# Decoder of two layers on one core: seven block products for the keys and values of the last cross-attention

## The chip, the cores and the metric

The kernel runs on one core of a Trainium2 chip. The metric is the device time of one execution in microseconds (us). TensorE (PE) multiplies matrices, its weight loads are listed apart as PEld; VectorE (DVE), ScalarE (ACT) and GpSimd (POOL) work on elements; SyncE (SP) issues most of the DMAs. All data is fp32.

## The reference

The input x has 8 batches of 256 tokens with 256 features. Two layers follow, each of a self-attention, a cross-attention and a feed-forward part with experts, each behind a layernorm and added to x:

```python
x = x + _L0_attn_ref(_layernorm(x), ...)
x = x + _L0_xattn_ref(ctx_2048, _layernorm(x), ...)
x = x + _L0_ffn_ref(_layernorm(x), ...)
x = x + _L1_attn_ref(_layernorm(x), ...)
x = x + _L1_xattn_ref(_layernorm(x), ctx_2048, ...)   # the change is here
x = x + _L1_ffn_ref(_layernorm(x), ...)

def _L1_xattn_ref(x, context, Wq, Wkv, null_kv, Wout, ln_scale, ln_bias):
    q = _split_heads(einsum('bnd,df->bnf', x, Wq))          # 16 heads of 64
    k, v = split(einsum('bmc,cf->bmf', context, Wkv), 2)    # context 256 x 512, Wkv 512 x 2048
    # a null key and value are put in front of k and v
    attn = softmax(einsum('bhid,bhjd->bhij', q * scale, k))
    out = einsum('bhij,bhjd->bhid', attn, v) @ Wout
    return (out - mu) * rsqrt(var + EPS) * ln_scale + ln_bias
```

The last part, `_L1_ffn_ref`, has one shared expert for all tokens and eight routed ones, of which each token takes the best.

## The kernel before

The program is unrolled. Up to about 620 us on the profile's clock it runs the first layer and the second layer's self-attention; then `null_cross_attention` (L1043) handles the cross-attention with heads of 64, one batch after another; from about 1173 us `token_experts` (L1273) runs the rest of the shared expert and the routed ones. The change lies in the middle part.

**Matmuls.** `product` (L272) splits the 128 output rows in two halves of 64 and issues a matmul for each, so its weight loads have 64 columns. In the trace each fp32 `nc.tensor.matmul` shows as two instructions.

**A batch b of the middle part.** A loop over b in `null_cross_attention` does the following.
- `weighted` (L1092) takes the keys kT, the values v and the queries qT of batch b. For each pair of heads it makes the scores (tile stx, in one of two double banks of the pool `scp`, tag "sc"), ACT takes their exponential into pTx (four buffers, tag "pT"), POOL adds two halves of it (both), TensorE sums these into the denominators (den) and multiplies pTx with the values (ox); ACT and DVE copy ox to oT.
- `layernorm_T` (L262) makes the transposed normed rows xnT of batch b+1, and `routed_norm` and `routed_rows` (L950, L964) those of batch b-1 for the experts; both end in transposes on TensorE and a copy on ACT.
- `reciprocals` (L1152) adds the null key's part to den, takes the reciprocal on DVE, writes it to DRAM (rd) and reads it back spread over the partitions (rs), both on SP's queue.
- `keys` (L1058) loads the transposed context ctxT of batch b+1 on SP's queue and multiplies it with the first half of wkv_x: for each two of the eight feature chunks, four contraction chunks with a moving operand of 256 tokens, and a copy of 512 columns on ACT (tile fm, kTx). `vals` (L1065) does it with the second half, context as weights and 512 features moving (vps, vx).
- `routed_scores` (L967) makes the routing scores of batch b-1.
- `divide` (L1184) multiplies oT by rs in four parts, two on POOL and two on DVE. `outward` (L1190) multiplies by Wout (tile wo), copies, normalises and adds to x, the last steps on DVE and POOL.
- `queries` (L1082) makes the null key's scores (nps) and the eight chunks of qT for batch b+1, copied by DVE.

Before the loop, keys, values and queries of batch 0 are made, and `load_shared` (L1222) loads the router and the shared expert's weights: `w_in` (L896) issues two DMAs on SP and a copy of the tail columns on POOL, `w_out` (L909) two DMAs, `ended` (L904) a memset on POOL. In batch 7 there are no keys to make: the weights wkv_x and wq_x are given up (`wproj.close()`), the tables of the routing are made on POOL, and the first quarter of the shared expert (tile hx) takes the place of keys and values.

**The order.** A planner (the tile framework) orders the instructions of each engine by priority, which is the order of the program text, and by its own estimate of when each can start. Within `tc.manual_schedule(engines=...)` the engines named keep the order of the text. Before, that holds for TensorE from batch 7 on (L1236). The planner also sets the waits: a write waits for earlier reads of the same tile where they overlap. TensorE's banks: `mm` has three single banks, `scp` two double ones, `op` one. Each engine handles its queue in order.

## Time and profile before

| | |
|---|---|
| Time, median of 3 runs | 1397.39 us (1395.36 to 1399.26) |
| The profiled execution, its own time | 1396.5 us |
| Its span, first to last instruction | 1394.8 us |
| TensorE busy | 97% of the span, 12198 matmul instructions |
| VectorE, ScalarE, GpSimd busy | 36%, 33%, 28% |
| Mean granted TensorE clock | 0.994 of full speed |
| The middle part, batch to batch | 63.7 us |

A line of the timeline has the start in us, the length in us of the merged run of instructions, the engine, the source line, the operation, output<-inputs by the names of the program, the shapes and the number of instructions; then, in brackets, how long the engine sat idle before it and what ended that. "128*64 128x256" on TensorE is a weight of 128 rows and 64 columns and 256 moving columns. The lengths of TensorE's runs include a modelled end of the last matmul, so neighbours overlap a little; differences of starts are free of that. A line that begins with a source line and ends in times "first to last" is from the view of one tile. PEclk is the granted clock in tenths, 9 for 90% or more, over 40 slices of the span.

### The profile page before, as it was taken

The numbers are of one execution on the slowest core, as the hardware profiler recorded it, in microseconds if no ns is written. First come the engines' busy times: TensorE is split into PE (matmuls) and PEld (weight loads), VectorE is DVE, ScalarE is ACT, GpSimd is POOL, SyncE is SP. The second block draws the span as 40 slices with busy tenths as digits, with TensorE's granted clock in tenths as the row PEclk, the third lists the DMA queues.
The fourth block names the chain that finished last, engine by engine and source line by source line (L and its number), as shares of the span: only waits on it lengthen the run. The fifth ranks groups of instructions, "written<-read, shape, count | busy, mean of one in ns | idle before, by whom it ended". The sixth has DMA issues, their size and how long they took to land.

```text
span 1394.8 us, 28640 instructions
## 1 busy us (share of the span) xinstructions
PE 1357.5 (97%) x12198; PEld 884.4 (63%) x12198; DVE 502.4 (36%) x1467; ACT 457.4 (33%) x730; POOL 395.7 (28%) x499
## 2 busy tenths in 40 slices
PE   6999999999999999989999999999999999999998
PEld 3666756756766666665655656565656555688884
DVE  5443563563565654330222213131312225422213
ACT  2555444444444434431222313131322222122221
POOL 4222142052033234220332415152423412400004
PEclk9999999999999999999999999999999999999999
DMA  8960000000000006010101010110101010779954
GB/s 312 345 205 16 9 24 9 8 24 1 1 9 2 2 9 221 1 53 26 32 16 31 16 47 2 46 32 16 32 1 32 1 31 5 283 289 414 402 209 127
DMA packets 46921, 116.56 MB, mean 84 GB/s; under 512 B 8273, under 2 KB 30401, under 8 KB 42433
## 3 DMA queue, kind: packets, MB, share of 16 engines
q1 hardware_dynamic: 38912, 92.74, 19.3%
q0 software_dynamic: 5152, 18.89, 3.6%
q10 hardware_dynamic: 2720, 3.02, 0.6%
q8 instruction: 98, 1.61, 0.5%
q14 instruction: 39, 0.31, 0.1%
HBM read 104.00 MB, written 27.93 MB: 95 GB/s over the span
## 4 chain that ended last, share of the span: by engine, by line
PE 85%; DVE 5%; POOL 4%; issue 1%; ACT 1%; DMA 0%; ACTq 0%; POOLq 0%; DVEq 0%; SPq 0%
PE fm L274 12%; PE st L332 9%; PE o L364 9%; PE vps L274 8%; PE h L274 6%; PE wo L274 4%; PE ox L1138 4%; PE stx L1100 4%; PE out L1475 3%; PE out L1292 3%; PE h L947 3%; PE qk L274 3%; PE hx L947 3%; PE tr L281 3%; PE den L1114 2%; PE ao L274 2%
## 5 line engine op out<-in xcount | busy, mean ns | idle before, releaser
L364 PE MATMUL o<-pT,padv 128*64 128x256 f32 (+1 forms) x1536 | 171.6, 365 | 1.1 <-POOL pT L344 1.1
L341 ACT ACTIVATE pT<-st 128x1024 f32<-128x1024 f32 (+1 forms) x128 | 110.5, 915 | 88.8 <-PE st L332 87.9
L364 PEld LDWEIGHTS o<-pT,padv 128*64 128x64 f32 x1536 | 103.1, 137 | 52.7 <-issue 10.0
L332 PE MATMUL st<-qm,kT 64*128 64x256 f32 (+1 forms) x1024 | 117.2, 367 | 0.9 <-DVE qm L310 0.6
L274 PE MATMUL fm<-ctxT,wkv_x 128*64 128x256 f32 x1024 | 112.9, 380 | 0.0
L274 PE MATMUL vps<-wkv_x,ctxT 128*64 128x512 f32 x512 | 111.8, 593 | 0.0
L332 PEld LDWEIGHTS st<-qm,kT 64*128 64x128 f32 x1024 | 90.1, 189 | 26.0 <-issue 15.6
L274 PEld LDWEIGHTS fm<-ctxT,wkv_x 128*64 128x64 f32 x1024 | 73.0, 137 | 37.3 <-issue 1.3
L1106 POOL TENSOR_TENSOR both<-pTx 128x512 f32<-128x512 f32 x64 | 79.6, 1273 | 57.4 <-ACT pTx L1104 33.8
L1104 ACT ACTIVATE pTx<-stx 128x1024 f32<-128x1024 f32 x64 | 62.1, 1021 | 89.9 <-PE stx L1100 86.8
L274 PE MATMUL h<-xrT,w 128*64 128x128 f32 (+1 forms) x1936 | 86.9, 250 | 1.4 <-issue 1.4
L274 PEld LDWEIGHTS h<-xrT,w 128*64 128x64 f32 x1936 | 84.3, 137 | 4.4 <-issue 2.1
L274 PEld LDWEIGHTS vps<-wkv_x,ctxT 128*64 128x64 f32 x512 | 36.4, 137 | 68.9 <-issue 68.6
L341 ACT ACTIVATE pT<-st,kbias 128x1024 f32<-128x1024 f32 x64 | 68.0, 1113 | 28.7 <-PE st L332 28.7
L256 POOL TENSOR_TENSOR lnrs<-lnve,mhalf 128x2 f32<-128x2 f32 x48 | 34.2, 717 | 147.0 <-DVE lnve L254 95.2
L332 PE MATMUL st<-qm,memk 64*128 64x256 f32 x512 | 68.8, 393 | 0.5
L939 ACT ACTIVATE sl<-h 128x128 f32<-128x128 f32 (+1 forms) x114 | 35.4, 310 | 96.1 <-PE h L274 56.7
L1100 PE MATMUL stx<-qTx,kTx 64*128 64x256 f32 x512 | 64.3, 391 | 2.5 <-ACT pTx L1104 2.5
L940 DVE TENSOR_TENSOR midr<-sl,h 128x128 f32<-128x128 f32 x102 | 29.4, 288 | 100.5 <-PE h L274 68.6
L251 DVE BATCH_NORM_STATS2 lxst<-yx 128x6 f32<-128x256 f32 x16 | 6.0, 418 | 162.7 <-ACT yx L1198 162.7
L274 PE MATMUL qk<-l_wqkv,xnT 128*64 128x512 f32 x256 | 62.6, 610 | 0.7 <-ACT xnT L284 0.7
L344 POOL TENSOR_SCALAR_AFFINE_SELECT pT<-pT 128x512 f32<-128x512 f32 x64 | 39.5, 638 | 83.1 <-ACT pT L341 79.8
(274 smaller groups left out, 2080.7 us busy)
## 6 DMA issues: line engine op xcount, KB each, us to landing
w<-packs SPq DMA_DIRECT2D x22, 1408.0 KB
w<-packs SPq DMA_DIRECT2D x22, 768.0 KB
rs<-rd SPq DMA_DIRECT2D x16, 512.0 KB
packs<-L_ffn_w_eDF SPq DMA_DIRECT2D x8, 704.0 KB
packs<-L_ffn_w_eDF SPq DMA_DIRECT2D x8, 640.0 KB
packs<-L_ffn_w_eFD SPq DMA_DIRECT2D x8, 640.0 KB
ctxT<-ctx_T SPq DMA_DIRECT2D x8, 512.0 KB
wkv_x<-L_xattn_Wkv POOLq DMA_DIRECT2D x1, 4096.0 KB, 17.3
```

The lines of the kernel that those rows point to most:

```text
L274: nc.tensor.matmul(out[h], lhsT[:, h], rhs, start=start, stop=stop, skip_group_check=True)
L281: nc.tensor.transpose(ps[:, c, t * P : (t + 1) * P], rows[:, t, c * P : (c + 1) * P], ident)
L332: nc.tensor.matmul(st[:, g, i, :n], kT[rows, c, bass.ts(kt, P)], qm[rows, 2 * mq + i, c, q0:], start=True, stop=True,)
L341: nc.scalar.activation(pT[:, :, :, :n], st[:, :, :, :n], AF.Exp, scale=scale, **kb)
L364: nc.tensor.matmul(o[64 * i : 64 * i + 64, mq, q0:], v_pad[:, kt, 4 * c + 2 * mq + i, 2 * g : 2 * g + 2, :], pTs[kt][:, g, i, : S - q0], s ...
L947: nc.tensor.matmul(h, shared["ws13"][:, c, lo : lo + P], shared["xnT"][:, c, bass.ts(q, 2 * S)], start=c == 0, stop=c == 1)
L1100: nc.tensor.matmul(st[:, g, kt, :], kT[rows, c, bass.ts(kt, P)], qT[rows, c, :], start=True, stop=True)
L1104: nc.scalar.activation(pT, st, AF.Exp, scale=scale)
L1106: nc.gpsimd.tensor_tensor(both, pT[:, :, 0, :], pT[:, :, 1, :], ALU.add)
L1138: nc.tensor.matmul(o[XD * g : XD * (g + 1), i, :], v[:, kt, 2 * (c2 + i) + g, :], pT[:, g, kt, :], start=kt == 0, stop=kt == 1, skip_group ...
L1292: nc.tensor.matmul(ps, mid[:, i, lo : lo + P], w2[:, i, :], start=i == 0, stop=i == NFC - 1)
L1475: nc.tensor.matmul(ps[h], mid[:, i, h], sets[k % len(sets)][1][:, i, :], start=i == 0, stop=i == NFC - 1, skip_group_check=True,)
```

## The change

For batches 1 to 7 the keys and the values are made by seven products of blocks in place of eight (Winograd's form of Strassen's scheme). The context is cut in two halves of tokens and two of its 512 features, each half of Wkv in two halves of its rows and two of its columns. Sums of the blocks of Wkv are made once by DVE, in 16 instructions of 512 columns, 12 of them behind batch 0's keys and 4 behind its queries; one overwrites a block of wkv_x. Sums of the blocks of ctxT are made by DVE for each batch, in four instructions of 256 columns (`sums_of_context`). `seven` makes the products in two banks xb and yb of one "sc" tile and a third bank zb from `mm`, so that three banks' sums serve four results: per seven, four copies on ACT (three into pT buffers, one into the result) and three adds on DVE. It is a generator that stops between products. For the keys a product is four feature chunks times two contraction chunks with 128 tokens moving; for the values, two contraction chunks with 512 features moving. Where a product writes one of xb and yb, `declare_no_dep` takes away the dependency on earlier reads of the other.

TensorE's order is now held to the text from the routed rows to the end of each batch, in every batch: the keys' product 1, the last two den sums (`rest`, split off from `weighted`), keys 2 and 5, 6, values 1, keys 7, keys 3 and 4, values 2 and 5, 6, the routed scores, nps, values 7, values 3 and 4, wo, queries. Batch 0's keys, values and queries are made as before. The context of batch b+1 is loaded ahead of `weighted`. The four divisions are all on POOL, but for batch 7. The shared expert's weights ws13 and ws2 are loaded in batch 7, after wkv_x is given up, ws2 behind `reciprocals`; the router stays at batch 0. The tiles rx, low and y have one buffer in place of two.

```diff
@@ -270,8 +270,10 @@
     def product(out, lhsT, rhs, start, stop):
-        for h in (slice(0, 64), slice(64, P)):
+        return [
             nc.tensor.matmul(out[h], lhsT[:, h], rhs, start=start, stop=stop, skip_group_check=True)
+            for h in (slice(0, 64), slice(64, P))
+        ]
     def transposed(rows, work, mm, tag, dst=None):
@@ -917,14 +919,17 @@
     norms = [(const.tile([P, 2, 2], F32, name=f"mean{b}"), const.tile([P, 2], F32, name=f"rstd{b}")) for b in range(B)]
     shared = {}
-    def load_shared():
+    def load_router():
         router = pool_s.tile([P, 2, E], F32, name="router")
         nc.gpsimd.dma_start(router, a["L1_ffn_router_DE"].rearrange("(c p) e -> p c e", p=P))
-        xnT = pool_s.tile([P, 2, B * S], F32, name="xnTe")
-        ws13 = w_in(pool_s, a["L1_ffn_ws1_DF"], a["L1_ffn_ws3_DF"], "ws13")
-        ws2 = w_out(ended(pool_s.tile([P, NFC, D], F32, name="ws2")), a["L1_ffn_ws2_FD"])
-        shared.update(router=router, xnT=xnT, ws13=ws13, ws2=ws2)
+        shared.update(router=router, xnT=pool_s.tile([P, 2, B * S], F32, name="xnTe"))
+    def load_shared(pool):
+        shared["ws13"] = w_in(pool, a["L1_ffn_ws1_DF"], a["L1_ffn_ws3_DF"], "ws13")
+        shared["mid_s"] = [ended(pool.tile([P, NFC, 2 * S], F32, name=f"mid{i}")) for i in range(2)]
+        shared["ws2"] = ended(pool.tile([P, NFC, D], F32, name="ws2"))
     def hidden(mid, first, n, pair, silu):
@@ -1040,27 +1045,145 @@
     def null_cross_attention(phase):
         work = phase.enter_context(tc.tile_pool(name="d2", bufs=2))
+        wsum = wproj.enter_context(tc.tile_pool(name="wsum", bufs=1, side="right"))
         scale = XD**-0.5
+        def feature(dst, w, rows, copy, c2):
+            n = w.shape[1]
+            ps = mm.tile([P, 2, S], F32, tag="mm", name="fm")
+            for i in range(2):
+                for cc in range(n):
+                    product(ps[:, i, :], w[:, cc, (c2 + i) * P : (c2 + i + 1) * P], rows[:, cc, :], cc == 0, cc == n - 1)
+            copy(dst[:, c2 : c2 + 2, :], ps)
...
+        def context(b):
+            t = ctxs.tile([P, CTX // P, S], F32, tag="ctxT", name="ctxT")
+            nc.sync.dma_start(t, a["ctx_T"][b].rearrange("(c p) t -> p c t", p=P))
+            return t
+        def keys(ctxT):
             kT = work.tile([P, nc8, S], F32, tag="kT", name="kTx", bufs=1)
             features(kT, wkv_x, ctxT, nc.scalar.copy)
-            return ctxT, kT
+            return kT
+        half = CTX // P // 2
+        def w_block(j, k):
+            return wkv_x.rearrange("p c (m k f) -> p c m k f", m=2, k=2)[:, half * j : half * (j + 1), :, k, :]
+        tw = wsum.tile([P, 3, half, 2, XH * XD // 2], F32, name="tw")
+        t1, t2, t3, t4 = tw[:, 0], tw[:, 1], w_block(0, 1), tw[:, 2]
+        def sums_of_weights(n):
+            dst, p, q = (
+                (t1, w_block(0, 1), w_block(0, 0)),
+                (t2, w_block(1, 1), t1),
+                (t4, w_block(1, 0), t2),
+                (t3, w_block(1, 1), w_block(0, 1)),
+            )[n]
+            for m in range(2):
+                for c in range(half):
+                    nc.vector.tensor_tensor(dst[:, c, m], p[:, c, m], q[:, c, m], ALU.subtract)
+        def sums_of_context(ctxT):
+            def block(i, j):
+                return ctxT[:, half * j : half * (j + 1), bass.ts(i, P)]
+            sw = wsum.tile([P, 3, half, P], F32, tag="sw", name="sw")
+            s1, s2, s3, s4 = sw[:, 0], sw[:, 1], block(1, 0), sw[:, 2]
+            nc.vector.tensor_tensor(s1, block(1, 0), block(1, 1), ALU.add)
+            nc.vector.tensor_tensor(s2, s1, block(0, 0), ALU.subtract)
+            nc.vector.tensor_tensor(s4, block(0, 1), s2, ALU.subtract)
+            nc.vector.tensor_tensor(s3, block(0, 0), block(1, 0), ALU.subtract)
+            return block(0, 0), block(0, 1), s4, block(1, 1), s1, s2, s3
+        w_terms = w_block(0, 0), w_block(1, 0), w_block(1, 1), t4, t1, t2, t3
+        def seven(terms, m, dst):
+            xy = scp.tile([P, 2, 2 * S], F32, tag="sc", name=f"kv{m}")
+            xb, yb = xy[:, 0], xy[:, 1]
+            read = {id(xb): [], id(yb): []}
+            def reads(bank, ins):
+                read[id(bank)].append(ins)
+                return ins
+            def product_of(n, bank, fresh):
+                s, t = terms[n - 1], w_terms[n - 1][:, :, m, :]
+                for i in range(4 if m == 0 else 1):
+                    for c in range(half):
+                        if m == 0:
+                            args = bank[:, bass.ts(i, P)], t[:, c, bass.ts(i, P)], s[:, c, :]
+                        else:
+                            args = bank, s[:, c, :], t[:, c, :]
+                        for made in product(*args, fresh and i == 0 and c == 0, c == half - 1):
+                            for other in (xb, yb):
+                                for ins in read[id(other)] if other is not bank else ():
+                                    tc.declare_no_dep(made.ins, ins.ins, reason="another bank")
+            if m == 0:
+                def of(i, j):
+                    return dst[:, 4 * j : 4 * j + 4, bass.ts(i, P)]
+                def seen(bank):
+                    return bank.rearrange("p (c t) -> p c t", c=4)
+            else:
+                def of(i, j):
+                    return dst[:, i, 8 * j : 8 * j + 8, :]
+                def seen(bank):
+                    return bank.rearrange("p (h d) -> p h d", h=8)
+            def kept(bank, name):
+                t = work.tile([P, 2 * S], F32, tag="pT", name=f"kv{name}{m}", bufs=4)
+                reads(bank, nc.scalar.copy(t, bank))
+                return seen(t)
+            product_of(1, xb, True)
+            p1 = kept(xb, "p")
+            yield
+            zb = mm.tile([P, 2 * S], F32, tag="mm", name=f"kvz{m}")
+            product_of(2, zb, True)
+            nc.vector.tensor_tensor(of(0, 0), p1, seen(zb), ALU.add)
+            product_of(5, yb, True)
+            p5 = kept(yb, "v")
+            yield
+            product_of(6, xb, False)
+            u = kept(xb, "u")
+            yield
+            product_of(7, xb, False)
+            reads(xb, nc.vector.tensor_tensor(of(1, 1), p5, seen(xb), ALU.add))
+            yield
+            product_of(3, yb, False)
+            reads(yb, nc.vector.tensor_tensor(of(0, 1), u, seen(yb), ALU.add))
+            product_of(4, xb, False)
+            nc.scalar.copy(of(1, 0), seen(xb))
+            yield
...
@@ -1080,14 +1203,19 @@
             return v
         def queries(xnT):
             nps = mm.tile([P, 2, S], F32, tag="mm", name="nps")
             for k in range(2):
                 product(nps[:, 0, :], wn[:, k].rearrange("p g w -> p (g w)"), xnT[:, k, :], k == 0, k == 1)
-            qT = work.tile([P, nc8, S], F32, tag="qT", name="qTx", bufs=1)
-            features(qT, wq_x, xnT, nc.vector.tensor_copy)
             en = work.tile([P, S], F32, tag="en", name="en")
             nc.scalar.activation(en, nps[:, 0, :], AF.Exp, scale=scale)
-            return qT, en
+            yield
+            qT = work.tile([P, nc8, S], F32, tag="qT", name="qTx", bufs=1)
+            for c2 in range(0, nc8, 2):
+                feature(qT, wq_x, xnT, nc.vector.tensor_copy, c2)
+                if c2 == 0:
+                    yield
+            yield qT, en
         def weighted(kT, v, qT):
@@ -1145,13 +1273,16 @@
                             )
                 (nc.vector.tensor_copy if c2 % 4 else nc.scalar.copy)(oT[:, c2 : c2 + 2, :], o)
                 before = [both for _, both in now]
-            for i, both in enumerate(before):
-                sums(nc8 - 2 + i, both)
-            return oT, den
+            def rest():
+                for i, both in enumerate(before):
+                    sums(nc8 - 2 + i, both)
+            return oT, den, rest
         def reciprocals(b, den, en):
-            r = work.tile([P, S], F32, tag="rx", name="rx")
+            r = work.tile([P, S], F32, tag="rx", name="rx", bufs=1)
             nc.vector.tensor_tensor(r, den, en, ALU.add)
             nc.vector.reciprocal(r, r)
             rd = dram.tile([2, nc8, S], F32, name=f"rd{b}")
...
@@ -1175,20 +1306,20 @@
...
-        def divide(oT, rs):
+        def divide(oT, rs, engines):
             for c2 in range(0, nc8, 2):
-                (nc.vector if c2 % 4 else nc.gpsimd).tensor_tensor(
+                engines[c2 % 4 // 2].tensor_tensor(
                     oT[:, c2 : c2 + 2, :], oT[:, c2 : c2 + 2, :], rs[:, c2 : c2 + 2, :], ALU.mult
                 )
...
@@ -1216,44 +1347,63 @@
         _, xnT = layernorm_T(0, work, mm)
-        ctxT, kT = keys(0)
+        ctxT = context(0)
+        kT = keys(ctxT)
+        for n in range(3):
+            sums_of_weights(n)
         v = vals(ctxT)
-        qT, en = queries(xnT)
-        load_shared()
+        *_, (qT, en) = queries(xnT)
+        sums_of_weights(3)
+        load_router()
         order = ExitStack()
         for b in range(B):
             more = b + 1 < B
-            oT, den = weighted(kT, v, qT)
+            if more:
+                ctxT = context(b + 1)
+            oT, den, rest = weighted(kT, v, qT)
             if more:
                 _, xnT = layernorm_T(b + 1, work, mm)
+                terms = sums_of_context(ctxT)
             else:
+                rest()
                 wproj.close()
                 late = ctx.enter_context(tc.tile_pool(name="mids", bufs=1, side="right"))
-                shared["mid_s"] = [ended(late.tile([P, NFC, 2 * S], F32, name=f"mid{i}")) for i in range(2)]
+                load_shared(late)
                 routing_tables(late)
                 order.enter_context(tc.manual_schedule(engines={mybir.EngineType.PE}))
             if b:
                 routed_rows(b - 1, routed_norm(b - 1, work), work)
+            if more:
+                order.enter_context(tc.manual_schedule(engines={mybir.EngineType.PE}))
+                kT = work.tile([P, nc8, S], F32, tag="kT", name="kTx", bufs=1)
+                v = work.tile([P, 2, XH, XD], F32, tag="vx", name="vx", bufs=1)
+                k7, v7, q = seven(terms, 0, kT), seven(terms, 1, v), queries(xnT)
+                next(k7)
+                rest()
             rs, old = reciprocals(b, den, en), en
             if b == 1:
                 in_range()
+            if not more:
+                w_out(shared["ws2"], a["L1_ffn_ws2_FD"])
             if more:
-                ctxT, kT = keys(b + 1)
-            if more:
+                for made in (k7, k7, v7, k7, k7, v7, v7):
+                    next(made)
                 if b:
                     routed_scores(b - 1)
-                v = vals(ctxT)
+                next(q)
+                next(v7)
+                next(v7)
             else:
                 for i, _ in enumerate(quarter(0)):
                     if i == 0:
                         routed_scores(b - 1)
-            divide(oT, rs)
+            divide(oT, rs, (nc.gpsimd, nc.gpsimd if more else nc.vector))
             outward(b, oT, old)
             if more:
-                qT, en = queries(xnT)
-        order.close()
+                *_, (qT, en) = q
+            order.close()
         with tc.manual_schedule(engines={mybir.EngineType.PE, mybir.EngineType.DVE}):
             for i, _ in enumerate(quarter(1)):
                 if i == 1:
```

More of the change, by code (lines that the diff above doesn't have):

```diff
@@ L1047, in features @@
         def features(dst, w, rows, copy):
-            n = w.shape[1]
             for c2 in range(0, nc8, 2):
-                ps = mm.tile([P, 2, S], F32, tag="mm", name="fm")
-                for i in range(2):
-                    for cc in range(n):
-                        product(
-                            ps[:, i, :], w[:, cc, (c2 + i) * P : (c2 + i + 1) * P], rows[:, cc, :], cc == 0, cc == n - 1
-                        )
-                copy(dst[:, c2 : c2 + 2, :], ps)
-        def keys(b):
-            ctxT = ctxs.tile([P, CTX // P, S], F32, tag="ctxT", name="ctxT")
-            nc.sync.dma_start(ctxT, a["ctx_T"][b].rearrange("(c p) t -> p c t", p=P))
+                feature(dst, w, rows, copy, c2)
@@ L1166, in reciprocals @@
             nc.gpsimd.tensor_tensor(en, en, r, ALU.mult)
-            low = work.tile([P, S], F32, tag="low", name="low")
+            low = work.tile([P, S], F32, tag="low", name="low", bufs=1)
             nc.vector.tensor_scalar(low, r, 1.0e-25, None, ALU.is_ge)
@@ L1177, in in_range @@
                 v = dens[:, k].rearrange("p t h -> p (t h)")
-                low = work.tile([P, S], F32, tag="low", name="lowk")
+                low = work.tile([P, S], F32, tag="low", name="lowk", bufs=1)
                 nc.vector.tensor_scalar(low, v, 1.0e-25, None, ALU.is_ge)
@@ L1190, in outward @@
         def outward(b, oT, en):
-            y = work.tile([P, 2, D], F32, tag="y", name="yx")
+            y = work.tile([P, 2, D], F32, tag="y", name="yx", bufs=1)
             ps = mm.tile([P, 2, D], F32, tag="mm", name="wo")
```

## The prediction

> **What bounds the kernel now.** I read the page first, then TensorE in order of time through one batch of the stage that is edited, then the other engines in the same stretch.
>
> ```profile
> PE 1357.5 (97%) x12198; PEld 884.4 (63%) x12198; DVE 502.4 (36%) x1467; ACT 457.4 (33%) x730; POOL 395.7 (28%) x499
> PEclk9999999999999999999999999999999999999999
> PE 85%; DVE 5%; POOL 4%; issue 1%; ACT 1%; DMA 0%; ACTq 0%; POOLq 0%; DVEq 0%; SPq 0%
> ```
>
> TensorE holds the chain that ended last for 85% of the span, at an ungated clock throughout. A busy share can hide slack in pipelined matmuls, so I look at start-to-start times:
>
> ```profile
> 741.57 14.03 PE L274 MATMUL fm<-ctxT,wkv_x 128*64 128x256 f32 x128
> 755.43 0.59 PE L274 MATMUL sc<-router,xnTe 128*64 128x8 f32 x16
> 755.87 13.93 PE L274 MATMUL vps<-wkv_x,ctxT 128*64 128x512 f32 x64
> 769.63 0.60 PE L274 MATMUL wo<-nvw,en 128*64 128x256 f32 x4
> ...
> 777.40 1.03 PE L274 MATMUL nps<-xnT,wn 128*64 128x256 f32 x8
> 778.26 7.08 PE L274 MATMUL fm<-xnT,wq_x 128*64 128x256 f32 x64
> 785.27 2.00 PE L1100 MATMUL stx<-qTx,kTx 64*128 64x256 f32 x16
> 787.59 2.05 PE L1100 MATMUL stx<-qTx,kTx 64*128 64x256 f32 x16 [0.32 <-ACT pTx L1104]
> ```
>
> Each group starts where the last one stops; the only wait named is 0.32 us, on an exponential. Keys (fm from ctxT) hold TensorE 755.43 - 741.57 = 13.86 us, or 108.3 ns for each of 128 instructions; values (vps) 769.63 - 755.87 = 13.76 us, 215.0 ns each of 64. The period is 63.7 us (741.57 to 805.26). Both are limited by columns: double the columns, double the time. So work removed here should come off the end, if nothing new is made to wait.
>
> **The products.** An nc.tensor.matmul of fp32 shows as two instructions, and the helper product issues two halves, so one product call is four instructions. For batches 1 to 7:
> - Keys before: 4 pairs of feature chunks x 2 x 4 contraction chunks = 32 calls, 128 instructions, 256 columns. After: 7 block products x 4 feature chunks x 2 contraction chunks = 56 calls, 224 instructions, 128 columns.
> - Values before: 16 calls, 64 instructions, 512 columns. After: 7 x 2 = 14 calls, 56 instructions, the same 512 columns.
>
> The values need no new rate: 56 x 215.0 = 12.04 us, a saving of 1.72. The keys need the rate at 128 columns with a weight load of 64 columns for each. The routed experts run just that form, in runs of two contraction chunks too:
>
> ```profile
> 1301.82 4.97 PE L274 MATMUL h<-xrT,w 128*64 128x128 f32 x88
> 1306.62 2.76 PE L1475 MATMUL out<-w,midr 128*64 128x256 f32 x24
> ...
> 1309.89 5.35 PE L274 MATMUL h<-xrT,w 128*64 128x64 f32 x176
> 1315.08 2.76 PE L1475 MATMUL out<-w,midr 128*64 128x256 f32 x24
> ```
>
> (1306.62 - 1301.82) / 88 = 54.5 ns. Keys after: 224 x 54.5 = 12.21 us, a saving of 1.65. Together 3.37 us a batch, **7 x 3.37 = 23.6 us**.
>
> Here a rule of the Trainium skill speaks against the change. "TensorE: Matmul & The Clock Gate", section "Back-to-back issue gap", says that a stream of weight loads and matmuls sustains about 81 ns a matmul at 128 columns, above the bare column time. By it the keys would cost 224 x 81 = 18.1 us, 4.3 more than now, and the change would lose 7 x (4.3 - 1.7) = 18 us. The trace disagrees: 54.5 ns at 128 columns, and 5.19 / 176 = 29.5 ns at 64 columns with equal loads, so at 128 the loads have room. I take 54.5; the ends are 54.2 (half of 108.3) and 55.1 (the run of that form from 1325.75 to 1330.60), 0.1 us a batch apart from it.
>
> **What TensorE now waits for.** Two readers must leave a bank before TensorE adds to it again. The order written out gives, from the first key product at 0: product 1 (1.74 us), the last den sums (0.9), products 2, 5, 6 (to 7.9), the values' 1, keys' 7, 3, 4 (to 14.8), values' 2, 5, 6 (to 20.0), scores and nps (to 21.3), values' 7, 3, 4 (to 26.4), then wo. An ACT copy of 512 columns takes 0.59 us and a DVE add with a PSUM operand about the 0.69 of the oT copy; with 0.1 to 0.25 us at each end that is about 1 us. Between each such read and the next write of its bank stand 3.5, 1.7 and 1.7 us of other products in the keys, and at least 5, 1.3 and 1.7 in the values. In batch 1 there are no scores, so one gap is 0.87. All are covered if the reader's queue is free. ACT makes eight copies before and after. DVE gains six adds (4.1 us) and four sums of the context (4 x 0.4), and loses two divisions (2.4); it is busy about 17 of 64 us. I book 0.1 us a batch, **+0.7**; the ends are 0 and, if each covered read came one DVE or ACT instruction late, about 0.5 a batch, 3.5.
>
> **Divisions and den.** Here is what they follow, one batch later:
>
> ```profile
> 868.10 0.42 DVE L1155 TENSOR_TENSOR rx<-den,en 128x256 f32<-128x256 f32 x1 [0.23 <-PE den L1114]
> ...
> 869.02 1.74 DVE L1156 RECIPROCAL rx<-rx 128x256 f32<-128x256 f32 x1
> ...
> 879.10 2.38 DVE L1186 TENSOR_TENSOR oT<-oT,rs 128x512 f32<-128x512 f32 x2 [7.02 <-DMA rs<-rd]
> ```
>
> ```profile
> 862.54 2.49 POOL L1106 TENSOR_TENSOR both<-pTx 128x512 f32<-128x512 f32 x2 [2.17 <-PE den L1114]
> 870.85 0.94 POOL L1166 TENSOR_TENSOR en<-en,rx 128x256 f32<-128x256 f32 x1 [5.81 <-DVE rx L1156]
> 879.15 3.46 POOL L1186 TENSOR_TENSOR oT<-oT,rs 128x512 f32<-128x512 f32 x2 [7.36 <-DMA rs<-rd]
> ```
>
> The division starts 11.1 us after den ends (867.99). A POOL division takes 1.73 us beside DVE's, and a sum of the same shape 1.25 alone. Four on POOL cost 5.0 alone, 6.9 at the shared rate. So wo is ready 16.1 to 18.0 us after den, while TensorE has 23.8 us of products (from 2.65 to 26.4). They stay **hidden**, with at least 5.8 us to spare; without that cover 1.6 to 3.4 us more than now would show. What queues on POOL behind the wait for rs is the norm after wo, needed later. DVE no longer waits for rs ahead of the adds. Moving den behind product 1 delays it 1.74 us, inside that margin.
>
> **Loads and sums, edits that hide.** The twelve early weight sums, 12 x 0.69 = 8.3 us on DVE, lie beside 27 us of batch 0's unchanged keys and values, where DVE sat idle for 29.5 us (its qTx row at 653.77); the last four lie beside its queries and scores. Uncovered they would cost their 11 us. The context's one DMA a batch is issued ahead of the scores instead of behind them; its slot was freed a batch earlier, so nothing on SP queues behind it. A seven holds a pair of score banks until its last read, at 15 and 27 on the clock above; the next scores ask for them after wo and the queries, at 41. The shared expert's weights move from batch 0 to batch 7:
>
> ```profile
> 621.29 0.37 SPq L899 DMA_DIRECT2D ws<-L_ffn_ws_DF  x1
> 621.70 0.47 SPq L900 DMA_DIRECT2D ws<-L_ffn_ws_DF  x1
> L901 POOL COPY ws<-ws x1: 287/287/287, 627.5 to 627.5; 128x128 f32<-128x128 f32 x1
> ```
>
> There the copy starts 6.2 us after the first issue. In batch 7 the space comes free when the queries end (1103.7 in today's times), the shared expert starts at 1123.2: 13 us of cover; all of it gone would show the 6.2. On SP they stand ahead of the rd and rs transfers by 0.84 us of issue; ws2's two issues come behind rs. The risk is POOL: its table work then ran 1105.64 to 1108.28, just ahead of the both sums, and a copy queued there that waits for its DMA until 1110 holds those sums, and behind them den and the reuse of pTx. I book **+0.5**, ends 0 and 2.5.
>
> **The sum.** -23.6 + 0.7 + 0.5 = -22.4 us. The profiled execution took 1396.5 us (span 1394.8 and 1.7 around it): 1374.1. It lies 0.9 under the median of 1397.4, for which the same difference gives **1375.0 us**.
>
> **Rivals.**
> 1. Partly covered, 1380 to 1392, say 1386: DVE or ACT is found busy when a bank must be read, or rs and four divisions come over 5.8 us later than now. 1.6 us a batch halves the gain. For it: the pinned order can't step aside, and every engine queue is in order. Against: DVE's and ACT's shares above.
> 2. Slower, 1414: the two banks are one tile, and if the declarations do not remove the waits between them, three products of each seven wait for a read of the other bank that was begun just ahead: 6 for the copy of bank y (0.9), 3 and 4 for the adds (1.0 each). That is 5.8 us a batch, 40.6 in all, against 23.6 gained. It decides from 3.37 of those 5.8 us, 58% of the waits. The edit then doesn't do what it says. Against: the exemption is written for each pair. No row of before can show it.
> 3. Short matmuls at the page's 81 ns: 1415; the expert rows speak against it.
>
> **How the numbers follow.** Likeliest 0.77, own range 1371 to 1380; rival 1 0.15; rival 2 0.05; rival 3 0.02; the rest, near no change, 0.01. A measurement of this kernel can tell about 0.3% from no change, 1393.2 to 1401.6. Faster: 0.77 + 0.15 = 0.92; same 0.02, with the edge of rival 1; slower 0.06. The low end is columns alone, without stalls and the kernel's 2 us of scatter: 1370.5; the high end takes the near half of rival 1: 1384.
>
> **What will show it.** Key products with 128 columns, 54 to 55 ns start to start, 12.2 us a batch; values 12.0; period near 60.4. No wait over 0.3 us before a product; wo straight behind the values; POOL's four divisions done some 5 us ahead. Waits named "ACT kv" or "DVE kTx/vx" of about 1 us ahead of products 3, 4 and 6 mean rival 2. A gap before wo with an oT releaser means rival 1. A POOL copy of ws amid the both sums shows the term of batch 7. A changed length of the stages before 620 or after 1170 would be outside this account and make it wrong.

## The result and the profile after

The changed kernel takes **1374.88 us** (median of 4 runs, 1374.21 to 1376.01) where the kernel before, run beside it, takes 1397.81 us (4 runs, 1395.36 to 1399.26). The ratio is **0.9839, 95% interval 0.9822 to 0.9856**, so 22.9 us are gone. The profiled execution took 1375.28 us with a span of 1373.6 us, 21.2 us less than the profiled one of before.

The page of the changed kernel: busy time of each engine (share of the span, number of instructions), the granted clock in 40 slices, and the engines' shares of the chain that ended last.

```profile
PE 1333.9 (97%) x12814; PEld 902.7 (66%) x12814; DVE 533.9 (39%) x1539; ACT 457.2 (33%) x730; POOL 404.6 (29%) x513
PEclk9999999999999999999999999999999999999999
PE 82%; DMA 6%; DVE 5%; POOL 3%; issue 1%; ACT 1%; SPq 1%; ACTq 0%; POOLq 0%; DVEq 0%
```

TensorE issues 616 more matmuls and is busy 23.6 us less: more, but shorter instructions. It still holds the chain, and the mean granted clock is 0.994 as before. The 6% of DMA in the chain are nearly all first loads of the program, before 86 us, through which the chain happens to be followed here.

TensorE in order of time through batch 1 of the edited stage (start, length, line, result and operands, shape, number of instructions, and in brackets an idle time with what ended it):

```profile
737.67 1.97 PE L274 MATMUL kv<-ctxT,wkv_x 128*64 128x128 f32 x32
739.47 1.03 PE L1242 MATMUL den<-both,hot 128*64 128x256 f32 x8
740.34 1.92 PE L274 MATMUL kvz<-ctxT,wkv_x 128*64 128x128 f32 x32
742.08 3.66 PE L274 MATMUL kv<-sw,tw 128*64 128x128 f32 x64
745.58 1.89 PE L274 MATMUL kv<-wkv_x,ctxT 128*64 128x512 f32 x8
747.29 1.92 PE L274 MATMUL kv<-ctxT,wkv_x 128*64 128x128 f32 x32
749.04 1.92 PE L274 MATMUL kv<-sw,wkv_x 128*64 128x128 f32 x32
750.79 1.92 PE L274 MATMUL kv<-ctxT,tw 128*64 128x128 f32 x32
752.53 1.89 PE L274 MATMUL kvz<-wkv_x,ctxT 128*64 128x512 f32 x8
754.25 3.60 PE L274 MATMUL kv<-tw,sw 128*64 128x512 f32 x16
757.68 0.59 PE L274 MATMUL sc<-router,xnTe 128*64 128x8 f32 x16
758.12 1.06 PE L274 MATMUL nps<-xnT,wn 128*64 128x256 f32 x8
759.01 1.89 PE L274 MATMUL kv<-wkv_x,ctxT 128*64 128x512 f32 x8
760.73 1.89 PE L274 MATMUL kv<-wkv_x,sw 128*64 128x512 f32 x8
762.45 1.89 PE L274 MATMUL kv<-tw,ctxT 128*64 128x512 f32 x8
764.16 0.60 PE L274 MATMUL wo<-nvw,en 128*64 128x256 f32 x4
...
798.07 1.97 PE L274 MATMUL kv<-ctxT,wkv_x 128*64 128x128 f32 x32
```

None of the products carries a bracket: nothing waits. Keys are the rows with 128 columns: (739.47 - 737.67) + (745.58 - 740.34) + (752.53 - 747.29) = 12.28 us for 224 instructions. Values are those with 512: 1.71 + 5.15 + 5.15 = 12.01 us for 56. Together 24.29, where keys and values took 27.62 before. wo follows the last value product at once. The period from batch to batch is 798.07 - 737.67 = **60.40 us**, 60.39 over the batches that follow; it was 63.69.

What TensorE waited for in the whole edited stretch, 600 to 1180 us (instruction, releaser: us in total, times, longest):

```profile
PE stx L1228 <- ACT pTx L1232: 2.5, 8, 0.3
PE tr L283 <- PE ao L274: 0.9, 1, 0.9
```

These and four smaller ones stood in the profile before as well. No wait on a bank, on a sum or on a division is among them. The least cover between a read and the next use of its bank is in batch 0's pass of the loop, where no routed scores stand between the values' products 6 and 7 (PEld is the weight load of product 7):

```profile
697.66 1.03 PE L274 MATMUL nps<-xnT,wn 128*64 128x256 f32 x8
698.57 0.20 PEld L274 LDWEIGHTS kv<-wkv_x,ctxT 128*64 128x64 f32 x4 [0.33 <-ACT kvu L1164]
698.57 1.94 PE L274 MATMUL kv<-wkv_x,ctxT 128*64 128x512 f32 x8
700.34 1.89 PE L274 MATMUL kv<-wkv_x,sw 128*64 128x512 f32 x8
```

Only nps stands between, 698.57 - 697.66 = 0.91 us. The weight load of product 7 waits 0.33 us for the copy of the bank, and product 7 takes 700.34 - 698.57 = 1.77 us where it takes 1.72 a batch later (759.01 to 760.73). So 0.9 us of other work is just too little, by some 0.05 us.

GpSimd in order of time, first in batch 1, then around the copy of the shared weights in batch 7:

```profile
751.74 4.97 POOL L1317 TENSOR_TENSOR oT<-oT,rs 128x512 f32<-128x512 f32 x4 [8.16 <-DMA rs<-rd]
...
1086.57 2.55 POOL L1234 TENSOR_TENSOR both<-pTx 128x512 f32<-128x512 f32 x2
1089.01 0.34 POOL L903 COPY ws<-ws 128x128 f32<-128x128 f32 x1
1089.26 5.00 POOL L1234 TENSOR_TENSOR both<-pTx 128x512 f32<-128x512 f32 x4
```

The four divisions end at 756.71, 7.45 us before wo begins. The copy stands amid the both sums as foreseen, but finds its data there and takes 0.34 us.

**Where the time came from.** From TensorE's first product of the stage to the first product of the shared expert (hx) the span lost 23.0 us: 622.44 to 1123.19 before, 622.62 to 1100.34 after. That is seven times 3.30. The part ahead is 0.2 us longer, and the part behind hx is 1.6 us longer, 273.2 us instead of 271.6, for a reason outside the change's own work. TensorE in order of time, in the routed experts, before:

```profile
1237.01 4.72 PE L274 MATMUL h<-xrT,w 128*64 128x64 f32 x156
1243.16 0.80 PE L274 MATMUL h<-xrT,w 128*64 128x64 f32 x20 [1.43 <-issue]
```

and after:

```profile
1219.31 1.03 PE L1625 MATMUL out<-w,midr 128*64 128x256 f32 x7
1221.69 2.10 PE L1625 MATMUL out<-w,midr 128*64 128x256 f32 x17 [1.36 <-issue]
...
1293.65 0.50 PE L274 MATMUL h<-xrT,w 128*64 128x64 f32 x9 [1.47 <-issue]
```

TensorE stops in the middle of a group for 1.4 us and waits for nothing of the program ("issue"). Before there is one such stop, after there are two. That is 1.4 of the 1.6 us. What they are comes at the end.

### The profile page after: what moved, and what is told of

It reads as the page before. It is cut to its first block, busy times and chain, and to the rows that moved or that the text cites. A ratio compares the mean times of both kernels' runs of the same rounds, so it can differ in the third digit from the quotient of the medians.

```text
span 1373.6 us, 30022 instructions
## 1 busy us (share of the span) xinstructions
PE 1333.9 (97%) x12814; PEld 902.7 (66%) x12814; DVE 533.9 (39%) x1539; ACT 457.2 (33%) x730; POOL 404.6 (29%) x513
## 4 chain that ended last, share of the span: by engine, by line
PE 82%; DMA 6%; DVE 5%; POOL 3%; issue 1%; ACT 1%; SPq 1%; ACTq 0%; POOLq 0%; DVEq 0%
PE kv L274 11%; PE st L334 8%; PE o L366 8%; PE h L274 6%; PE fm L274 5%; PE wo L274 5%; PE ox L1266 4%; PE stx L1228 4%; PE out L1625 3%; PE out L1442 3%; PE h L952 3%; PE qk L274 3%; PE hx L952 3%; PE tr L283 2%; PE den L1242 2%; PE ao L274 2%
## 5 line engine op out<-in xcount | busy, mean ns | idle before, releaser
L1266 PE MATMUL ox<-pTx,vx 128*64 128x256 f32 x512 | 61.1, 381 | 0.0
L1228 PEld LDWEIGHTS stx<-qTx,kTx 64*128 64x128 f32 x512 | 46.1, 186 | 20.3 <-issue 9.2
L274 PE MATMUL wo<-wout_x,oT 128*64 128x256 f32 x512 | 58.0, 379 | 0.0
L334 PEld LDWEIGHTS st<-qm,memk 64*128 64x128 f32 x512 | 48.0, 186 | 15.1 <-issue 5.1
L274 PE MATMUL fm<-xnT,wq_x 128*64 128x256 f32 x512 | 57.0, 379 | 0.0
```

Source lines behind the costliest of these rows:

```text
L274: nc.tensor.matmul(out[h], lhsT[:, h], rhs, start=start, stop=stop, skip_group_check=True)
L334: nc.tensor.matmul(st[:, g, i, :n], kT[rows, c, bass.ts(kt, P)], qm[rows, 2 * mq + i, c, q0:], start=True, stop=True,)
L1228: nc.tensor.matmul(st[:, g, kt, :], kT[rows, c, bass.ts(kt, P)], qT[rows, c, :], start=True, stop=True)
L1266: nc.tensor.matmul(o[XD * g : XD * (g + 1), i, :], v[:, kt, 2 * (c2 + i) + g, :], pT[:, g, kt, :], start=kt == 0, stop=kt == 1, skip_group ...
```

## The experiments

The later runs were made on other chips, on which the kernel before takes 1399.5 to 1400.8 us. Each is therefore set against the kernel before on its own chip, by the ratio, and for small effects by the period of the edited stage.

**Do the declarations take waits away that would have cost more than the products gain?** (rival 2)

```
-                            for other in (xb, yb):
-                                for ins in read[id(other)] if other is not bank else ():
-                                    tc.declare_no_dep(made.ins, ins.ins, reason="another bank")
+                            pass
```

> The changed kernel without the declarations, so that each product also waits for the last read of the other bank. Theory of the columns with covered waits (the forecast): the declarations matter, since products 6, 3 and 4 of each seven would wait for a read begun just ahead. From the changed kernel's own rows: a copy of the bank ends about 0.97 us after the product that it follows could have been followed, an add about 1.08 us; 2 x (0.97 + 1.08 + 1.08) = 6.3 us a batch, period 66.7 us, 1375 + 7 x 6.3 = 1419 us, slower than the kernel before. Rival (the reads are over anyway, the declarations do nothing): 1375 us, period 60.4.

Measured: 1421.15 us, ratio 1.0146 (1.0129 to 1.0163), period 66.49 us. The waits of TensorE, in the same columns as above:

```profile
PE kv L274 <- ACT kvv L1162: 10.4, 14, 0.7
PE kv L274 <- DVE vx L1178: 6.0, 7, 0.9
PE kv L274 <- DVE kTx L1178: 6.0, 7, 0.9
PE kv L274 <- DVE vx L1181: 5.5, 7, 0.8
PE kv L274 <- DVE kTx L1181: 5.5, 7, 0.8
```

They are the three waits in each seven that the rival named, on a read of the other bank. Six a batch cost 6.10 us in period, 1.02 us each. The view shows only 33.4 us of idle time for all 42, 0.80 each: the period, not the idle time, gives the price. So the rival described the kernel without its declarations rightly, and its 5.8 us a batch was near. Products and declarations belong together: seven products without them lose 20 us against the kernel before.

**Is it the interleaving of keys and values that covers the real bank waits?** All seven key products in a row, then all seven for the values:

```
-                for made in (k7, k7, v7, k7, k7, v7, v7):
+                for made in (k7, k7, k7, k7, v7, v7, v7, v7, v7):
                     next(made)
                 if b:
                     routed_scores(b - 1)
                 next(q)
-                next(v7)
-                next(v7)
```

> The changed kernel with all seven products of the keys in a row and then all of the values, so that product 7 directly follows product 6 in both. Covered-waits theory: product 7 must then wait for the ACT copy of its own bank, about 0.96 us twice a batch, 1375 + 13.4 = 1388 us, with waits named ACT ahead of product 7. Rival (the sequencing costs nothing, or the copy is faster than a product can be issued): 1375 us.

Measured: 1390.8 us, ratio 0.9931 (0.9915 to 0.9948), period 62.31 us, so 1.92 us a batch more. One wait has come to the list of TensorE's waits:

```profile
PE kv L274 <- ACT kvu L1164: 10.4, 14, 0.7
```

Two a batch, the read of a bank just ahead of the product that adds to it again. In the changed kernel's order one product of 1.7 us stands between them in the keys, and in the values the routed scores and nps, 759.01 - 757.68 = 1.33 us; both are enough to hide a read. Without them more than half of the gain is lost.

**Is the gain the columns alone?** Eight products in place of the sevens, all other edits kept (order pinned, den behind the first group, divisions on GpSimd, loads moved). The sums of weights and contexts are left out with the sevens.

```
-                k7, v7, q = seven(terms, 0, kT), seven(terms, 1, v), queries(xnT)
+                k7, v7, q = eight_keys(ctxT, kT), eight_values(ctxT, v), queries(xnT)
```

> The changed kernel with keys and values again by the eight products of before (256 and 512 columns, copies by ACT), all else kept: order, den behind the first group of keys, divisions on GpSimd, context loaded early, shared expert's weights in batch 7. Theory (all of the gain is columns): 1397 us within 2, period 63.7. Rival (order, divisions or loads give part of the gain): below 1393 us; (the late load of the weights costs): above 1399 us.

Measured: 1401.91 us, ratio 1.0008 (1.0001 to 1.0015), period 63.69 us as before. In the profiled execution the stage lasts 500.74 us from its first product to hx (625.06 to 1125.80), against 500.75 before. So in the stage everything but the products and their sums is worth nothing; the ratio leaves a loss of about 1 us, which then lies outside it.

Then sevens for one half only, with `seven(terms, 0, kT), eight_values(ctxT, v)` for the keys alone, and `eight_keys(ctxT, kT), seven(terms, 1, v)` for the values alone. Only that half's sums of weights are made, and one sum of the context gets a buffer of its own, since the other half still needs the block that it would overwrite.

> The changed kernel with sevens for the keys alone; the values by eight products as before. Theory of the columns: the keys take 224 x 54.5 = 12.2 us in place of 13.9, so 7 x 1.65 = 11.5 us of the 23: 1386 us, period 62.1. By the page's 81 ns for 128 columns: slower, 1397 + 7 x 4.3 = 1427 us.

> The changed kernel with sevens for the values alone; the keys by eight products as before. Theory of the columns: 7 x 1.72 = 12.0 us: 1386 us, period 62.0. Together with the keys alone it should add up to the whole gain within 2 us; if waits in one seven were covered only by the other's products, the two parts would add up to less than the whole.

Measured: keys alone 1388.37 us, ratio 0.9922 (0.9907 to 0.9937), period 62.11, that is 1.58 us a batch; values alone 1387.31 us, ratio 0.9906 (0.9891 to 0.9921), period 61.98, 1.71 us a batch. Their sum is 3.29, the whole change's 3.30. The halves add up, so neither spends a cover that the other needs.

**Do short products cost extra?** (rival 3) The kernel before, with the columns of its keys cut in two, the same arithmetic in twice as many instructions:

```
+                    for t in range(2):
+                        cols = bass.ts(t, P)
...
+                                ps[:, i, cols], w[:, cc, (c2 + i) * P : (c2 + i + 1) * P], rows[:, cc, cols], cc == 0, cc == n - 1
```

> The kernel before with one edit: the keys' eight products have 128 tokens moving in place of 256, twice as many matmuls, in all eight batches. By the routed experts' row (54.5 ns): 256 x 54.5 = 13.95 us a batch against 13.86, 1398.5 us, the same within the measurement. By the page's 81 ns: 20.7 us a batch, 1397 + 8 x 6.9 = 1452 us.

Measured: 1400.85 us, ratio 1.0003 (0.9994 to 1.0011), period 63.85. TensorE in order of time:

```profile
744.94 14.19 PE L274 MATMUL fm<-ctxT,wkv_x 128*64 128x128 f32 x256
758.97 0.59 PE L274 MATMUL sc<-router,xnTe 128*64 128x8 f32 x16
```

(758.97 - 744.94) / 256 = 54.8 ns an instruction. At 81 ns they would have held TensorE for 20.7 us. Doubling the instructions costs 0.16 us a batch and no more.

**How much cover do the divisions have?** First two of the four put back on the vector engine:

```
-            divide(oT, rs, (nc.gpsimd, nc.gpsimd if more else nc.vector))
+            divide(oT, rs, (nc.gpsimd, nc.vector))
```

> The changed kernel with the four divisions two on GpSimd and two on DVE, as before the change, in every batch. Forecast's theory: the divisions are hidden on either engine, so 1375 us within 1.5, period 60.4. Rival (the division on DVE, waiting for rs, holds the adds behind it on DVE and through them the banks): the values' first add comes late, product 4 of a seven waits, up to 1 to 3 us a batch, 1382 to 1396 us.

Measured: 1377.57 us, ratio 0.9837 (0.9821 to 0.9854), period 60.39. Where the divisions run neither costs nor saves.

Then GpSimd gets eight, or twelve, more operations of the same shape in batches 0 to 6: each divided part has rs added and taken away again, so the result differs only by rounding.

```
+                if engines[1] is nc.gpsimd:
+                    for op2 in (ALU.add, ALU.subtract) * (2 if c2 < 4 else 1):
+                        nc.gpsimd.tensor_tensor(oT[:, c2 : c2 + 2, :], oT[:, c2 : c2 + 2, :], rs[:, c2 : c2 + 2, :], op2)
```

This is the twelve; the eight do it once for each part.

> The changed kernel with eight more GpSimd operations of a division's size in batches 0 to 6, an addition and a subtraction of rs behind each division, so the last part of oT is ready 10 us later. The forecast gave the divisions at least 5.8 us of cover and would show 7 x (10 - 5.8) = 29 us at most, 1404 us. The changed kernel's trace gives more: the divisions end 7.45 us ahead of wo, and wo needs the last part only 3 us after its start; by that 10 us just fit, 1375 to 1377 us.

> The same with twelve more operations a batch, 15 us. By the trace's 10.5 us of cover 4.5 us a batch come out, 1375 + 7 x 4.5 = 1406 us, slower than the kernel before, with a wait of wo for POOL oT. If the divisions were hidden behind something that grows with them (no fixed cover), 1375 us.

Measured for eight: 1376.58 us, ratio 0.9844 (0.9827 to 0.986), period 60.39. Some 10 us a batch are hidden whole. Only one batch shows the edge of the cover, in TensorE's order of time:

```profile
1007.00 1.08 PE L274 MATMUL wo<-wout_x,oT 128*64 128x256 f32 x8 [0.33 <-POOL oT L1322]
```

Measured for twelve: 1423.08 us, ratio 1.018 (1.0161 to 1.0198), with periods of 66.4 to 68.0 us. The last 5 us of work a batch cost 46.5 us against the eight, half as much again as the 31 that were expected. TensorE's list of waits, and its order of time in one batch:

```profile
PE wo L274 <- POOL oT L1322: 29.9, 7, 4.8
```

```profile
769.25 1.90 PE L274 MATMUL wo<-wout_x,oT 128*64 128x256 f32 x16
775.18 3.68 PE L274 MATMUL wo<-wout_x,oT 128*64 128x256 f32 x16 [4.04 <-POOL oT L1322]
778.65 1.07 PE L274 MATMUL wo<-nvw,en 128*64 128x256 f32 x4
```

The waits are 29.9 us, as foreseen. But behind the wait sixteen instructions that took 1.90 us take 3.68. The table by stretches shows why (stretch, length, busy time and instructions of PE, PEld, DVE, ACT and POOL, granted clock, share of DMA, GB/s):

```profile
772.00:774.00 2.00, 0.00 (x0) 0.00 (x0) 0.79 (x1) 0.00 (x0) 2.00 (x3) 0.87 0.15 53
774.00:776.00 2.00, 0.82 (x4) 0.53 (x6) 0.00 (x0) 0.00 (x0) 2.00 (x2) 0.50 0.00 0
...
778.00:780.00 2.00, 2.00 (x14) 1.05 (x12) 0.00 (x0) 0.00 (x0) 0.00 (x0) 0.50 0.00 0
780.00:782.00 2.00, 2.00 (x20) 1.29 (x18) 0.00 (x0) 0.00 (x0) 0.00 (x0) 0.92 0.00 0
```

The granted clock, 1.00 until the wait, falls to 0.50 near 773.5 us and stays there for 6.8 us. The same follows each of the seven waits, for 3.4 or 6.8 us. In the seven stretches at half clock TensorE works for 30.5 us in all (the same view in steps of 0.25 us). Half of that, 15.3 us, is lost, and so explains nearly all of the other 16.6 of the 46.5 us.

**A version that goes further.** Batch 0 by sevens too. The weight sums that the keys need come first, and the order is pinned there as well:

```
-        kT = keys(ctxT)
-        for n in range(3):
-            sums_of_weights(n)
-        v = vals(ctxT)
-        *_, (qT, en) = queries(xnT)
-        sums_of_weights(3)
-        load_router()
+        terms = sums_of_context(ctxT)
+        for m in range(2):
+            for n in (0, 1, 3, 2):
+                sums_of_weights(n, m)
...
+        k7, v7, q = seven(terms, 0, kT), seven(terms, 1, v), queries(xnT)
+        for made in (k7, k7, k7, v7, k7, k7, v7, v7, q, v7, v7):
+            next(made)
...
+        load_router()
```

> The changed kernel with batch 0 by sevens too: DVE makes the weights' sums in the order in which the products want them (0.6 us each, keys' half first), while products 1 and 2, which need none, run. Theory of the columns: one more batch saves 3.4 us, and product 1 can fill TensorE's waits at the end of the last self-attention (0.6, 0.7 and 0.9 us): 1370 to 1372 us. Rival (the sums come late, as 16 x 0.6 = 9.8 us must be done in about 10 us): TensorE waits up to 4 us in batch 0, 1374 to 1376 us.

Measured: 1373.51 us, ratio 0.982 (0.9804 to 0.9836). That is above the 1370 to 1372 us of the theory, and against the changed kernel's 0.9839 it left open whether this version is faster, so both were timed once more on one chip:

> The changed kernel again, beside the kernel before on one chip, as the partner of the version whose batch 0 also goes by sevens. Nothing is edited. Period 60.4 us, ratio 0.984.

> Batch 0 by sevens too, timed again beside the changed kernel on the same chip. If the saved two products (3.3 us) less the waits seen in the first run (0.7 for the keys' half, 0.9 ahead of a transpose) survive, it is 2 to 4 us below the changed kernel, ratio about 0.982. The rival, that the work ahead of batch 0 only waits elsewhere, gives the changed kernel's own ratio, 0.984.

Measured: the changed kernel 1377.92 us (5 runs, 1377.45 to 1380.94), ratio 0.9847 (0.9833 to 0.986); with batch 0 by sevens **1373.60 us** (5 runs, 1372.51 to 1375.77), ratio **0.9811 (0.9798 to 0.9824)**. The intervals do not meet. The first scores of batch 0 begin at 656.15 instead of 658.95, and hx at 1097.82 instead of 1100.26. So the batch is worth 2.4 to 2.8 us, and the rest of the 4.3, 1.9 us, lies behind hx. The "issue" stops of this pair, which sum to 1.96 and 2.86 us there, explain 0.9 of it; the other 1.0 is open. TensorE in order of time in that version shows what two of its new places cost:

```profile
623.65 0.41 PE L283 MATMUL tr<-ident,xn 128*128 128x128 f32 x2 [0.94 <-DVE xn L260]
...
636.08 1.97 PE L274 MATMUL kv<-ctxT,tw 128*64 128x128 f32 x32 [0.69 <-DVE kTx L1179]
```

The first replaces a wait of 0.90 us that stood at the same place. The second is new, and the vector engine in order of time tells why:

```profile
633.55 1.28 DVE L1102 TENSOR_TENSOR tw<-wkv_x,tw 128x512 f32<-128x512 f32 x2
634.75 0.67 DVE L1171 TENSOR_TENSOR kTx<-kvp,kvz 128x512 f32<-128x512 f32 x1
635.35 0.68 DVE L1179 TENSOR_TENSOR kTx<-kvv,kv 128x512 f32<-128x512 f32 x1
```

The add that frees the bank (L1179) stands in the queue behind the weight sums (L1102), which here must be done in the first batch that uses them. It is the vector engine found busy that rival 1 spoke of, once, at 0.7 us.

What the pin of TensorE's order is worth alone was not run; with eight products it was worth nothing.

## Why the prediction was right, step by step

- **The products, -23.6 us: right.** Keys 12.28 us against 12.21, values 12.01 against 12.04, 3.33 us a batch in batch 1 against 3.37. Over the stage 23.0 us are gone. The rate at 128 columns is 54.4 to 54.7 ns start to start (740.34 to 742.08 holds 32, 742.08 to 745.58 holds 64), against 54.5; with the first product's slower start it is 54.8 over the 224. Keys alone and values alone give it in halves.
- **The rule that spoke against it (rival 3): refuted by experiment, for this form.** In the eight-product keys with half the columns the instruction took 54.8 ns, and the period grew by 0.16 us. The 81 ns of the Trainium skill's "TensorE: Matmul & The Clock Gate", section "Back-to-back issue gap", would have made it grow by 6.9. For fp32 with loads of 64 columns the column time sets the pace at 128 columns here.
- **Waits on banks, +0.7: mis-sized, 0 measured but for 0.05 us.** The cover counted out by hand held, so the low end of the bounds was the value; the one gap of 0.9 us was just too short. The serial order shows that it was cover and not an absence of need: 1.92 us a batch without it.
- **Divisions and den, hidden: right, with the cover sized too small.** "At least 5.8 us" took 6.9 us for the four divisions, which took 4.97, and all four divided parts as needed when wo begins. In fact wo begins with a product that needs no division, and then takes the parts one after the other. Some 10 us more work was hidden and 15 was not. With that cover gone the price was more than the late time: the clock added half as much again.
- **Early weight sums, context load, score banks, all booked at nothing: right.** The kernel with eight products and all these edits but the sums has the old period and the old stage to 0.01 us. The sums themselves stand in the changed kernel, whose list of waits shows none for them.
- **Copy of the shared weights in batch 7, +0.5: mis-sized, 0 measured.** It takes 0.34 us between two sums and nothing behind it is late; the shared expert starts straight behind.
- **Rival 1 did not happen.** The vector and scalar engines read every bank in time, but for those 0.05 us; only the version with batch 0 by sevens has such a place. **Rival 2** is what the kernel would be without the declarations, 6.10 us a batch instead of 5.8. The declarations do what they say.
- **"A changed length of the stages after 1170 would be outside this account": this happened, by 1.6 us.** In the profiled pair it took back part of the stage's 23.0; the medians differ by 22.9 all the same. The sum of -22.4 thus came out near with a stage gain 0.6 us larger and a term that it did not have: 1374.1 us forecast for the profiled execution and 1375.3 measured, 1375.0 for the median and 1374.9 measured. The columns and the hidden work were foreseen; that the median was met within 0.1 us is luck, since two terms that were not there (+1.2) stood against a loss behind hx that was not forecast, and the four runs scatter over 1.8 us.
- **Two slips without effect.** The low end of 1370.5 does not follow from the terms named with it: 1396.5 - 23.6 - 2 is 1370.9. And "an ungated clock throughout" holds for the edited stage, not for the whole span; why the row of digits can't show it comes below.

## What to carry to other kernels

Where TensorE is limited by columns and its neighbours have room, one block product in eight can be dropped, and the gain is the column time of that product. The waits that it makes must all be either declared away (a read of another bank, about 1.0 us each) or covered by other work of TensorE between a read and the bank's next use (1.3 us were enough here, 0.9 just not). Left bare, 1.9 us of such waits a batch took more than half of the gain, and 6.1 us made it a loss. Count the price of a stall from start to start rather than from its idle time, and remember that one of over 2 us can cost clock as well.

## What the hardware showed that was not expected

**A pause of TensorE can be paid twice.** Pauses of 0.7 to 0.9 us, six a batch in the kernel without declarations, left the granted clock of that stage at 1.00. One pause of 3.3 to 4.8 us a batch brought it to 0.50 for 3.4 or 6.8 us, seven times out of seven. Sizes between them stand in all fourteen profiles, in the first layer, near 201 and 307 us. Before the change, in TensorE's order of time and in the view by stretches:

```profile
201.19 0.44 PE L281 MATMUL tr<-ident,qkr 128*128 128x128 f32 x2 [2.54 <-DVE qkr L463]
```

```profile
200.00:201.00 1.00, 0.00 (x0) 0.00 (x0) 0.56 (x1) 0.00 (x0) 0.40 (x1) 1.00 0.38 130
202.00:203.00 1.00, 1.00 (x11) 0.46 (x13) 0.51 (x1) 0.25 (x1) 0.00 (x0) 0.50 0.00 0
```

Of these 28 pauses of 2.2 to 2.8 us, 19 took the clock to 0.50, for 3.4 us each (once 6.8), and nine did not, one of 2.70 us among them. The stops of 1.1 to 1.6 us behind hx never did. But in the profile of the eight products with the pinned order it fell at 621 us behind two pauses of 0.6 and 0.7 us close together. The section "The HAM clock gate (the "warmup" mystery)" of the Trainium skill's "TensorE: Matmul & The Clock Gate" gives an idle window of about 3.4 us for this. The fall lasts one or two times that length here, but a single pause of that length is not needed; what decides for the shorter ones is not shown. A digit of PEclk covers 35 us, and 3.4 us at half clock leave it at 0.95, which prints as 9.

**TensorE stops for over 1 us where nothing in the program holds it.** Every profile listed here has one or two such stops of 1.1 to 1.6 us behind hx, in the routed experts, and some have shorter ones of 0.3 to 0.8 us besides; which instruction they hit moves from kernel to kernel. In both profiles of the first pair a 16 KB transfer on the instruction queue (q8 of the page) begins about 2.4 us before work resumes (1240.75 for the stop that ends at 1243.16; 1219.26 and 1291.16 for 1221.69 and 1293.65). The same holds, at 2.2 to 2.5 us, for each of the 23 stops of 0.5 us or more in the routed experts of all fourteen profiles; for three of 0.8 us in the shared expert it does not. But behind hx there are 24 such transfers before and 25 after, and most go by without a stop, so their number doesn't explain why there are two stops in place of one. That the stop is TensorE waiting for its own instructions behind the expert weights, which arrive at some 400 GB/s in that stage, is argued from this coincidence; no run took the traffic away to show it. It bounds how closely a sum like this one can be held: 1.4 us from a place that the change doesn't touch.
